# The norm of the product in eight parts, placed among the output units

## The chip, the cores and the metric

The kernel runs on one core of a Trainium2 chip. The metric is device microseconds of one execution. The kernel before takes 1781.53 us (median of three runs, 1780.02 to 1782.26).

The core has a matrix engine (PE, whose weight loads are shown apart as PEld), a vector engine (DVE), a scalar engine (ACT), a general engine (POOL) and a queue engine (SP) that only issues transfers. POOL and ACT can issue transfers too. Each engine takes its instructions in the order in which the program recorded them.

## The reference

Two layers act on a 512 x 512 picture with 64 channels. The first is a gated triangle product with a norm before it and another behind it; the second a spectral convolution with 12 x 12 modes, each on a group-normed input and added to it:

```python
x = x + _L0_conv_ref(_gn(x), ...)
x = x + _L1_conv_ref(_gn(x), L1_conv_w_real, L1_conv_w_imag)
```

What matters here is the end of the first layer:

```python
m = sequence_mask.astype(xn.dtype)
mask = (m[:, :, None] * m[:, None, :])[..., None]
...
out_gate = jax.nn.sigmoid(xn @ ogate_w + ogate_b)
out = jnp.einsum('bkjd,bkid->bijd', left, right)
out = _ln(out, onorm_w, onorm_b)
out = out @ out_w + out_b
return out * out_gate
```

The mask is zero or one for each row. Where a column is masked, the product is zero, its norm is zero and the value before the gate is the bias row alone. So the kernel ranks the rows and columns, keeps the at most 256 unmasked ones first, and computes the product for those only (the branch `compact`).

## The kernel before, in words

`compact` goes through these stages. Rows of x are gathered in ranked order and their sums taken; the two sides of the product are computed and written to `left_d` and `right_d`; the product is made for one channel after another and written to `tri_d` (64 channels x 256 x 256); then comes the loop over steps that the change touches; then the spectral part and the last stage, which adds the second layer and writes the output.

The loop over steps handles two kinds of units of eight steps each, in a hand-written order that every engine follows (`manual_schedule`).

- A **part** is an eighth of the norm of the product with its output projection. The eight parts come first (`first = 8`). A step reads half of a tile of `tri_d` (read through SP into four places, L1025), multiplies it on PE with `both`, a 64 x 128 matrix that holds the centring matrix and the output weights side by side (L1058, two instructions for each of eight matmuls, as 64 of the 128 rows each), squares the centred half on ACT (L1078) and copies the projected half to SBUF on ACT (L1079). DVE sums the squares for two steps (L1083), ACT takes the root (L1089), DVE the reciprocal (L1263) and multiplies (L1271). POOL adds the bias row (L1278), and SP writes 8 columns of the result to `u_d` (L1283), four times a part.
- An **output unit** is 32 columns of x for half of the rows, 2 MB, gathered by POOL in two transfers (L638 is the line of every gather). There are 32, two for each of 16 column groups `jc`: one for the masked rows' half (`half` 1) and one for the other. A step transposes four blocks on PE (L1038), ACT adds a mean (L1040), PE centres them (`center_x`, `c_ps`, L1045), ACT squares (L1076), DVE sums (L1083), and twelve steps behind the centring PE multiplies by the gate's weights (`gate_x`, `w_ps`, L1045), DVE multiplies by the reciprocal (L1274) and adds the gate's bias (L1280). ACT takes the sigmoid (L1221), POOL multiplies by u or by the bias row (`gated`, L1109) and adds to x (`added`, L1113), and SP stores the result into `x_h` (L1129). One unit later DVE takes the statistics for the second group norm (L1168), and PE the forward transform of the columns (L1140), whose result ACT copies (L1148) and SP writes to `modes_d`.

The loop runs transposes 13 steps ahead (`LEAD`) of the multiply by the gate's weights. At its head stands each step's PE work; x is held in five places (`RING`), z in four buffers.

u is what `u_d` holds for an output unit's 32 columns. `load_u` issues 32 reads of 64 KB in one go (L1100), each for one column whose number, a slot, is read from `slot_row` into a register of SP. The reads for the first column group go out at the step at which the first output unit begins, those for the next ones one column group ahead. A masked column's slot is at least the number of unmasked ones; slots over K = 256 are cut to K, where `u_d` holds the bias row, and below K the parts write the bias row there, the product being zero.

A reciprocal for unit or part k + 1 (L1263) is DVE's in the last step of unit k, so two of them in a row enclose eight steps.

Of the kernel before, what the change touches and what calls it, by code (L numbers as in the profile page):

```python
# [9 lines left out]
F32 = mybir.dt.float32  # L10
I32 = mybir.dt.int32
# [6 lines left out]
P = 128  # L18
# [28 lines left out]
def conv_preact_kernel(ctx: ExitStack, tc: tile.TileContext, t: dict):  # L47
# [24 lines left out]
    n_i = const.tile([1, 1], I32, name="n_i")  # L72
    with tc.tile_pool(name="ix", bufs=1) as xp, tc.tile_pool(
# [30 lines left out]
        nc.vector.tensor_copy(n_i, cum[0:1, 7:8])  # L104
        rest = xp.tile([P, 4], F32, name="rest")
# [515 lines left out]
    def compact(fc):  # L621
# [209 lines left out]
        with tc.tile_pool(name="tri", bufs=1) as trp:  # L831
# [10 lines left out]
            with tc.tile_pool(name="mk", bufs=1) as mk, tc.tile_pool(name="mkp", bufs=1, space=PSUM) as mps:  # L842
# [5 lines left out]
                nc.vector.tensor_copy(mask_s, mask_ps)  # L848
                own = mk.tile([P, 2, P], F32, name="own")
# [3 lines left out]
                nc.vector.tensor_reduce(mask_own, own, AX.X, ALU.add)  # L853
            with tc.tile_pool(name="ti", bufs=5) as ip, tc.tile_pool(name="tt", bufs=3) as tp, tc.tile_pool(
# [49 lines left out]

                for c in range(4):
                    load_sides(c)
                for c in range(-2, C):
                    if c + 2 < C:
                        turn_sides(c + 2)
                    if 0 <= c + 1 < C:  # L910
                        keep_sides(c + 1)
                    if c >= 0:
                        product(c)
                    if 4 <= c + 6 < C:
                        load_sides(c + 6)

            SIZE = 8
            LEAD = 13
            RING = 5
            first = K * 2 // 64  # L920

            units = [(jc, half) for jc in range(NJ) for half in ((1, 0) if jc < NJ - 1 else (0, 1))]
            total_g = (first + len(units)) * SIZE
            with tc.manual_schedule(), tc.tile_pool(name="late", bufs=1) as lp:
# [13 lines left out]

                order = (0, 1, 3, 4, 2)

                def place(i):
                    return places[:, i * 64 * C : (i + 1) * 64 * C].rearrange("p (n c) -> p n c", c=C)
# [47 lines left out]
                with tc.tile_pool(name="np_x", bufs=LEAD + 2) as tp, tc.tile_pool(name="np_q", bufs=2) as sqp, tc.tile_pool(  # L990
# [3 lines left out]
                ) as s1, tc.tile_pool(name="np_n", bufs=1, space=PSUM) as ps_n, tc.tile_pool(name="opf", bufs=1, space=PSUM) as ps_f, ExitStack() as products:  # L994

                    ps_y = products.enter_context(tc.tile_pool(name="np_b", bufs=2, space=PSUM))
                    ps_c = ps_w = None

                    both = lp.tile([P, P], F32, name="both")
                    for h in range(2):  # L1000
                        hs = slice(h * C, (h + 1) * C)
                        nc.vector.tensor_copy(both[hs, :C], center[hs, hs])
                        nc.vector.tensor_copy(both[hs, C:], weights["out"][hs, hs])
# [6 lines left out]

                    factors = [scratch[:, i, SIZE * 8 :] for i in range(2)]
# [5 lines left out]
                    products_t = [place(6).rearrange("p n c -> p (n c)")[:, i * 2 * N : (i + 1) * 2 * N] for i in range(4)]  # L1017

# [3 lines left out]
                    def load_product(q):  # L1022

                        for h in range(2):
                            nc.sync.dma_start(  # L1025
                                products_t[q % 4][h * C : (h + 1) * C],
                                tri_d.rearrange("c j i -> c (j i)")[:, (2 * q + h) * 2 * N : (2 * q + h + 1) * 2 * N],
                            )

                    def transpose(s):  # L1030
                        k, n = divmod(s, SIZE)
                        if k < first:
                            return
                        flat = x_of(k - first).rearrange("p n c -> p (n c)")
# [13 lines left out]
                    def centered(s):  # L1048
                        if s >= first * SIZE:
                            return times(ps_c, "c_ps", s, center_x)  # L1050

                        ps = ps_y.tile([P, 2, 4, P], F32, name="y_ps")
                        q, e = divmod(s, 2)
                        of = products_t[q % 4][:, e * N : (e + 1) * N].rearrange("p (i k) -> p i k", i=4)
                        for i in range(4):
                            for h in range(2):
                                hs = slice(h * C, (h + 1) * C)
                                nc.tensor.matmul(ps[:, h, i, :], of[hs, i, :], both[hs], start=True, stop=True)  # L1058

                        xts[s] = tp.tile([P, 4, P], F32, name="xt_c")  # L1060
                        return ps

                    def raw(s):
                        return xts[s].rearrange("p h (i c) -> p (h i) c", c=C).rearrange("p (h i) c -> p h i c", h=2)

                    def of_pair(t, e):

                        return t.rearrange("p (h e i) c -> p h e i c", h=2, e=2)[:, :, e]

                    def squared(s, cps):  # L1070
# [4 lines left out]
                        if s >= first * SIZE:  # L1075
                            nc.scalar.activation(sq, cps, AF.Square)  # L1076
                        else:
# [456 lines left out]
```

## Time and profile before

| what | value |
|---|---|
| time, median of three runs | 1781.53 us (1780.02 to 1782.26) |
| the profiled execution: its own time | 1777.78 us |
| the profiled execution: its span | 1776.0 us |
| mean granted PE clock | 0.891 |
| PE, DVE, ACT, POOL busy over the span | 88%, 80%, 53%, 53% |
| first joined matmul of the norm of the product | 624.6 us after the span's start |
| first and last centring matmul of the output units | 730.5 and 1415.6 us |
| DVE's reciprocals: 32 for output units | 0.535 us each, 748.0 to 1426.6 us |
| HBM traffic over the span | 311.60 MB read, 204.60 MB written, 291 GB/s |

A line of the timeline gives the start and the length of a run of like instructions, engine, line, operation, tiles (written <- read), shape and number; brackets give the idle time before it and what ended it. The lengths of pipelined instructions overlap: what one costs an engine that is never idle is read from start to start. A line with SPq is SP's queue: the time of issuing, not of moving the data. In a table of windows, the busy time of each engine is followed by the number of its instructions; a DMA share of 1 means that the 16 DMA engines had packets all the time.

### The profile page before, as it was taken

To read this page: it belongs to the slowest core of one execution; us is meant where nothing else is said; L and a number is where in the kernel's file an instruction comes from. 1 tells how busy PE (TensorE), PEld (TensorE's weight loads), DVE (VectorE), ACT (ScalarE), POOL (GpSimd) and SP (SyncE) were. 2 spreads that over 40 slices of the span, in tenths; PEclk is the share of its full clock that TensorE was granted. 3 is DMA by queue.
4 is the path that set the end of the run, shared out by engine and by line. 5 is a ranking of instruction groups with operands and counts; after the bars stand their busy time and mean duration, and the time that the engine had idled before them with its cause. 6 is when DMAs were issued, how large, how long until landed. Compare 5 with 4: busy or idle time off the path is not lost. (4 is left out here: it accounts for less than half of the span.)

```text
span 1776.0 us, 32619 instructions
## 1 busy us (share of the span) xinstructions
PE 1567.8 (88%) x10918; PEld 1242.0 (70%) x10918; DVE 1413.7 (80%) x2982; ACT 933.0 (53%) x1660; POOL 936.5 (53%) x695
## 2 busy tenths in 40 slices
PE   6779799997999978899999999999999977998772
PEld 5667666662899867787888888888888745665341
DVE  7989678887455568688999999999999984865451
ACT  3666566663333266676777777777777742011000
POOL 4666211111000037698999999999999881111110
PEclk9999999999899999899999999999999976555555
DMA  7999278878898789868767767776776699999999
GB/s 281 386 386 388 107 206 227 229 229 245 279 305 303 257 246 347 298 196 296 265 242 257 253 233 259 264 249 239 249 264 244 212 318 400 425 427 427 426 427 385
DMA packets 192593, 518.48 MB, mean 292 GB/s; under 512 B 37664, under 2 KB 104480, under 8 KB 151456
## 3 DMA queue, kind: packets, MB, share of 16 engines
q1 hardware_dynamic: 156112, 295.65, 47.5%
q0 software_dynamic: 32832, 218.45, 33.4%
q10 hardware_dynamic: 3472, 2.20, 0.5%
q8 instruction: 89, 1.46, 0.3%
q14 instruction: 88, 0.72, 0.1%
HBM read 311.60 MB, written 204.60 MB: 291 GB/s over the span
## 5 line engine op out<-in xcount | busy, mean ns | idle before, releaser
L1045 PE MATMUL w_ps<-gate_x,xt_c 128*128 128x128 f32 x2048 | 280.5, 281 | 30.0 <-DVE z_t L1274 28.6
L1113 POOL TENSOR_TENSOR places<-places,z_t 128x1024 f32<-128x1024 f32 x127 | 301.3, 2372 | 8.0
L1045 PEld LDWEIGHTS w_ps<-gate_x,xt_c 128*128 128x128 f32 x2048 | 252.0, 194 | 46.4 <-DVE z_t L1274 44.6
L1045 PE MATMUL c_ps<-center_x,xt_c 128*128 128x128 f32 x2048 | 277.0, 279 | 0.8 <-ACT xt_c L1040 0.4
L1045 PEld LDWEIGHTS c_ps<-center_x,xt_c 128*128 128x128 f32 x2048 | 252.8, 194 | 3.8 <-ACT xt_c L1040 3.0
L1440 PE MATMUL l_ps<-places,rinv 24*128 24x512 f32 x512 | 206.2, 1118 | 29.3 <-DVE places L1447 19.0
L1168 DVE BATCH_NORM_STATS2 stats2c<-places 128x6 f32<-128x128 f32 x1024 | 220.5, 278 | 9.9 <-POOL places L1113 9.9
L1083 DVE TENSOR_REDUCE scratch<-sq_c 128x16 f32<-128x1024 f32 x160 | 194.6, 1216 | 31.1 <-ACT sq_c L1078 16.1
L1221 ACT ACTIVATE z_t<-z_t 128x1024 f32<-128x1024 f32 x128 | 135.5, 1058 | 131.8 <-DVE z_t L1280 131.1
L1440 PEld LDWEIGHTS l_ps<-places,rinv 24*128 24x128 f32 x512 | 119.8, 302 | 110.8 <-DVE places L1447 56.9
L1278 POOL TENSOR_TENSOR z_t<-z_t,bias_row_out 128x1024 f32<-128x1024 f32 x32 | 75.6, 2363 | 226.3 <-PE y_ps L1058 202.1
L1040 ACT ACTIVATE xt_c<-t_ps,ab_xc 128x512 f32<-128x512 f32 x256 | 176.0, 688 | 11.5 <-PE t_ps L1038 10.6
L1274 DVE TENSOR_TENSOR z_t<-w_ps,rs_n 128x512 f32<-128x512 f32 x256 | 172.0, 672 | 6.2 <-PE w_ps L1045 6.1
L1076 ACT ACTIVATE sq_c<-c_ps 128x512 f32<-128x512 f32 x256 | 150.8, 589 | 31.4 <-PE c_ps L1045 30.8
L1280 DVE TENSOR_TENSOR z_t<-z_t,scratch 128x1024 f32<-128x1024 f32 x128 | 156.3, 1221 | 9.9 <-ACT rs_n L1089 3.7
L688 DVE BATCH_NORM_STATS2 stats1c<-x_ps 128x6 f32<-128x512 f32 x256 | 157.1, 682 | 7.7 <-PE x_ps L687 7.4
L1109 POOL TENSOR_TENSOR z_t<-z_t,places 128x1024 f32<-128x1024 f32 x64 | 151.8, 2371 | 14.6 <-ACT z_t L1221 14.4
L1038 PE MATMUL t_ps<-c_ident,places 128*128 128x128 f32 x1024 | 158.4, 278 | 0.0
L1038 PEld LDWEIGHTS t_ps<-c_ident,places 128*128 128x128 f32 x1024 | 118.5, 142 | 51.4 <-issue 51.4
L1447 DVE TENSOR_TENSOR places<-places,l_ps 128x512 f32<-128x512 f32 x176 | 109.3, 682 | 55.2 <-DMA places<-x_h,dst_i 42.1
L1109 POOL TENSOR_TENSOR z_t<-z_t,bias_row_out 128x1024 f32<-128x1024 f32 x63 | 149.4, 2372 | 5.8 <-ACT z_t L1221 5.5
L673 ACT COPY xc<-xg 128x128 f32 x352 | 105.0, 298 | 66.1 <-POOL xc L673 47.1
(214 smaller groups left out, 2557.0 us busy)
## 6 DMA issues: line engine op xcount, KB each, us to landing
x_h<-places SPq DMA_DIRECT2D x64, 1024.0 KB
out_x<-places SPq DMA_DIRECT2D x44, 1024.0 KB
places<-u_d SPq DMA_DIRECT2D x512, 64.0 KB
out_x<-lx_t SPq DMA_DIRECT2D x20, 1024.0 KB
rbc<-rs_d POOLq DMA_DIRECT2D x32, 512.0 KB, 7.1
left_d<-o_c SPq DMA_DIRECT2D x64, 256.0 KB
right_d<-o_c SPq DMA_DIRECT2D x64, 256.0 KB
left_raw<-left_d SPq DMA_DIRECT2D x64, 256.0 KB
```

The costliest lines, as they stand in the source:

```text
L688: nc.vector.bn_stats(stats[:, 0, 16 * (jc % quarter) + 4 * r + c, :], ps.rearrange("p i k -> p (i k)"))
L1038: nc.tensor.transpose(tps[:, i, :], flat[:, o : o + P], ident)
L1040: nc.scalar.activation(xts[s], tps, AF.Identity, bias=ab1[:, 2:3])
L1045: nc.tensor.matmul(ps[:, 2 * i : 2 * i + 2, :], xts[s][:, i, :], w, start=True, stop=True)
L1076: nc.scalar.activation(sq, cps, AF.Square)
L1083: nc.vector.tensor_reduce(totals[k % 2][:, 8 * (n - 1) : 8 * (n + 1)], sqs.pop(s // 2), AX.X, ALU.add)
L1109: nc.gpsimd.tensor_mul(zs[k, c], zs[k, c], u)
L1113: nc.gpsimd.tensor_add(xr, xr, zs.pop((k, c)))
L1168: nc.vector.bn_stats(st[k // 4][:, g, k % 4, :], x_of(k)[:, :, 2 * g : 2 * g + 2])
L1274: nc.vector.tensor_mul(z[:, 8 * odd : 8 * odd + 8, :], wps, rs)
L1280: nc.vector.tensor_add(z, z, bias_ps["ogate"].unsqueeze(1).to_broadcast([P, 16, C]))
L1440: nc.tensor.matmul(ps.rearrange("p j o -> p (j o)"), rinv[h, b, :], it[h], start=True, stop=True, tile_position=(32 * g, 0),)
```

## The change

The eight parts no longer form a stage of their own. The units of the loop stand in a list, `line`: output unit 0, parts 0, 1 and 2, output units 1, 2 and 3, part 3, output units 4 and 5, part 4, and so on, two output units to a part, up to part 7; then the other output units. The number of steps stays the same.

A part now goes through the same operations as an output unit, from the centring on. Its data come from `tri_d` through SP straight into the ring of `xt_c` tiles (17 instead of 15), 128 KB a transfer and two a step, 15 steps ahead (`EARLY`), with no transpose. The joined matrix is gone: the centring and the output weights are two matmuls over 128 rows each (L1045 of before, `times`), 12 steps apart, and the copy by ACT is gone. DVE multiplies from PSUM.

u's reads are planned (`plan_u`), two columns in each step, for 16 steps. A plan begins four steps into the slot behind the part that makes the last of the column group's u, or behind the output unit that frees the place. Since parts can now follow reads, a masked column must read the bias row whatever its slot: slots from the number of unmasked rows on are set to K. The first output unit's x is gathered in the stage of the product.

```diff
+    n_f = const.tile([1, 1], F32, name="n_f")
...
+        nc.vector.tensor_copy(n_f, cum[0:1, 7:8])
...
+                past = mk.tile([1, N], I32, name="past")
+                nc.vector.tensor_scalar(past, slot_row, n_f, float(K), ALU.is_ge, ALU.mult)
+                nc.vector.tensor_max(slot_row, slot_row, past)
...
+            line = [0, "p0", "p1", "p2"]
+            for k in range(1, len(units)):
+                line.append(k)
+                if k % 2 == 1 and k > 1 and 2 + k // 2 < PARTS:
+                    line.append(f"p{2 + k // 2}")
...
+                def load_first(r):
+                    jc, half = units[0]
+                    dst = place(order[0])[:, r * JC : (r + 1) * JC].rearrange("p j c -> p (j c)")
+                    nc.vector.memset(dst[:, :1], 0.0)
+                    gather(dst, tiles, src_i, 2 * half + r, jc)
...
+                    if c in (C // 2, 3 * C // 4):
+                        load_first(c // (3 * C // 4))
...
+                    def load_product(s):
+
+                        xts[s] = tp.tile([P, 4, P], F32, name="xt_c")
+                        o = (part_of[s // SIZE] * SIZE + s % SIZE) // 2 * 4 * N + s % 2 * N
                         for h in range(2):
                             nc.sync.dma_start(
-                                products_t[q % 4][h * C : (h + 1) * C],
-                                tri_d.rearrange("c j i -> c (j i)")[:, (2 * q + h) * 2 * N : (2 * q + h + 1) * 2 * N],
+                                xts[s][h * C : (h + 1) * C].rearrange("p i k -> p (i k)"),
+                                tri_d.rearrange("c j i -> c (j i)")[:, o + 2 * h * N : o + (2 * h + 1) * N],
                             )
...
-                        ps = ps_y.tile([P, 2, 4, P], F32, name="y_ps")
...
-                        for i in range(4):
-                            for h in range(2):
-                                hs = slice(h * C, (h + 1) * C)
-                                nc.tensor.matmul(ps[:, h, i, :], of[hs, i, :], both[hs], start=True, stop=True)
...
-                            nc.scalar.activation(of_pair(sqs[s // 2], n % 2), cps[:, :, :, :C], AF.Square)
-                            nc.scalar.copy(raw(s), cps[:, :, :, C:])
+                        nc.scalar.activation(sq, cps, AF.Square)
...
-                    def load_u(jc):
+                    waiting = []
+
+                    def plan_u(jc):
+
+                        def some(k, regs=[]):
+                            if k % 16 == 0:
+                                regs[:] = slots_of(mybir.EngineType.SP, jc, k, k + 16)
+                            for j in range(k, k + 2):
+                                slot = regs[j % 16]
+                                nc.sync.dma_start(us[jc][:, j], u_d[:, bass.ds(slot, 1)].rearrange("p o r c -> p (o r) c"))
+
                         us[jc] = place(5 + jc % 2).rearrange("p (j r) c -> p j r c", r=2)
-                        for j, slot in enumerate(slots_of(mybir.EngineType.SP, jc)):
-                            nc.sync.dma_start(us[jc][:, j], u_d[:, bass.ds(slot, 1)].rearrange("p o r c -> p (o r) c"))
+                        waiting.extend(lambda k=k: some(k) for k in range(0, JC, 2))
...
+                    for u in range(1, len(units)):
+                        at_k = max(at[u] - 3, at[u - 5] + 2 if u >= 5 else 0)
+                        loads[at_k * SIZE + 3], loads[at_k * SIZE + 6] = (u, 0), (u, 1)
...
+                    for jc in range(NJ):
+                        after = [parts_at[min(jc, PARTS - 1)]] + [at[units.index((jc - 2, 0))] for _ in range(jc >= 2)]
+                        plans.setdefault((max(after) + 1) * SIZE + 4, []).append(jc)
...
                         if 0 <= s < total_g:
-                            wps = raw(s) if k < first else times(ps_w, "w_ps", s, gate_x)
+                            wps = times(ps_w, "w_ps", s, gate_x if k in unit_of else weights["out"])
                             del xts[s]
                         if 0 <= s + LEAD - 1 < total_g:
-                            cps = centered(s + LEAD - 1)
+                            one = center_x if (s + LEAD - 1) // SIZE in unit_of else center
+                            cps = times(ps_c, "c_ps", s + LEAD - 1, one)
...
-                        if s == first * SIZE:
-                            load_u(0)
-                        if n == 4 and v % 2 == 0 and 0 <= v < len(units) - 2:
-                            load_u(v // 2 + 1)
+                        for jc in plans.get(s, ()):
+                            plan_u(jc)
+                        if waiting:
+                            waiting.pop(0)()
```

In the list, a unit's place is its slot: output unit 0 is slot 0, part 2 slot 3, output unit 1 slot 4, part 3 slot 7, output units 4 and 5 with part 4 slots 8 to 10, output unit 12 slot 20. Slot k holds steps 8k to 8k + 7. u's columns 16 to 31 for the first column group are read in steps 28 to 35, and POOL's second multiply of output unit 1 takes them in step 37.

## The prediction

> **What bounds the kernel now.** I read the stretches first, then the four engines' timelines, then SP's.
>
> Two windows, one in the product's norm and one in the output stage. Columns: window, length, busy time (instructions) of PE, PEld, DVE, ACT, POOL, granted clock, DMA share, GB/s.
>
> ```profile
> 670.00:700.00 30.00, 24.24 (x318) 21.02 (x315) 26.01 (x32) 21.10 (x43) 22.87 (x10) 1.00 1.02 347
> 950.00:1000.00 50.00, 47.79 (x397) 42.74 (x397) 49.01 (x116) 36.04 (x55) 47.45 (x23) 0.97 0.72 246
> ```
>
> The norm stage is full on the DMA engines (1.02); the output stage has DMA room (0.72) but none on DVE (98%), POOL and PE (95%). The change moves work from the first into the second.
>
> The DVE timeline: two steps of an output unit, then four reciprocals (L1263), each the last step of a slot.
>
> ```profile
> 904.17 0.87 DVE L1168 BATCH_NORM_STATS2 stats2c<-places 128x6 f32<-128x128 f32 x4
> 904.96 1.21 DVE L1083 TENSOR_REDUCE scratch<-sq_c 128x16 f32<-128x1024 f32 x1
> 906.08 0.68 DVE L1274 TENSOR_TENSOR z_t<-w_ps,rs_n 128x512 f32<-128x512 f32 x1
> 906.68 0.86 DVE L1168 BATCH_NORM_STATS2 stats2c<-places 128x6 f32<-128x128 f32 x4
> 907.46 0.67 DVE L1274 TENSOR_TENSOR z_t<-w_ps,rs_n 128x512 f32<-128x512 f32 x1
> 908.16 1.22 DVE L1280 TENSOR_TENSOR z_t<-z_t,scratch 128x1024 f32<-128x1024 f32 x1
> ...
> 641.62 0.56 DVE L1263 RECIPROCAL scratch<-rs_n 128x64 f32<-128x64 f32 x1
> 747.97 0.54 DVE L1263 RECIPROCAL rs_n<-rs_n 128x64 f32<-128x64 f32 x1
> 1010.18 0.54 DVE L1263 RECIPROCAL rs_n<-rs_n 128x64 f32<-128x64 f32 x1
> 1426.65 0.53 DVE L1263 RECIPROCAL rs_n<-rs_n 128x64 f32<-128x64 f32 x1
> ```
>
> No gaps: by starts, stats 0.79, reduce 1.12, multiplies 0.60 and 0.70, bias 1.13, so 5.12 us per two steps and, with the reciprocal, 20.95 a unit. From 641.62 to 747.97 eight parts take 106.4 us (13.3 each); units 0 to 11 take 262.2 to 1010.18. Together 368.6.
>
> PE's timeline: end of the product, a part's joined matmuls, a unit's step.
>
> ```profile
> 612.54 5.51 PE L895 MATMUL tri_c_ps<-right_t,left_t 128*128 128x256 f32 x24
> ...
> 709.00 2.05 PE L1058 MATMUL y_ps<-both,places 64*128 64x128 f32 x30 [0.24 <-DMA places<-tri_d]
> ...
> 915.40 1.06 PE L1045 MATMUL w_ps<-gate_x,xt_c 128*128 128x128 f32 x8
> 916.30 1.06 PE L1045 MATMUL c_ps<-center_x,xt_c 128*128 128x128 f32 x8
> 917.19 0.60 PE L1038 MATMUL t_ps<-c_ident,places 128*128 128x128 f32 x4
> ```
>
> Joined: 2.05/30 = 68 ns an instruction. Full-height: 0.90/8 = 112 ns.
>
> SP's queue: last write of tri_d and first read of it, last write of u_d and first read of it, then a run of u reads.
>
> ```profile
> 619.00 0.32 SPq L903 DMA_DIRECT2D tri_d<-tri_t  x1
> 621.08 22.04 SPq L1025 DMA_DIRECT2D places<-tri_d  x20
> ...
> 751.98 0.33 SPq L1283 DMA_DIRECT2D u_d<-z_t  x1
> 759.68 0.36 SPq L1100 DMA_DIRECT2D places<-u_d  x1
> ...
> 899.79 13.33 SPq L1100 DMA_DIRECT2D places<-u_d  x22
> ```
>
> A read of what was just written goes out 2.1 us (256 KB, quiet) to 7.7 us later (512 KB, others ahead); a u read costs SP 13.33/22 = 0.61 us.
>
> **The change part by part.** Removed: 64 ACT copies (L1079, 0.58 us each) and the joined matrix. ACT is 72% busy (36.04/50), so I take 0; no more than their 37 us could come back, and none while DVE sets the pace.
>
> PE per part: 16 x 8 x 68 ns = 8.7 us becomes 8 steps x (0.90 + 0.89) = 14.3. A unit is 8 x (0.90 + 0.89 + 0.44) + two transforms of 1.0 = 19.8. DVE per part: 4 x (1.12 + 0.60 + 0.70) + 0.45 = 10.1. POOL: the groups' 2.37 us go at starts 2.39 apart, so 4 x 2.39 = 9.6 a part, 8 x 2.39 and two gathers of 1.0 = 21.1 a unit. Two units and a part: PE 53.9, DVE 52.0, POOL 51.8. Before, they cost 2 x 20.95 + 13.3 = 55.2. PE now leads, so there is almost nothing to gain; I take 54.5 (PE's sum, and 55.4 if the longest engine of each slot counts: 17.0, 18.6, 19.8).
>
> The Trainium skill, "TensorE: Matmul & The Clock Gate", section "Back-to-back issue gap", gives 81 ns a matmul at 128 columns in real streams. By that a part would be 10.4 us on PE, DVE would lead at 52.0, and five groups would save another 12 us; the f32 rows here show 112 ns.
>
> Fill: PE ends the product at 618.05. Unit 0 is already there: 8 steps of 1.33 us (t and c) and one more, then four c of 0.9 for part 0, whose data can land at 624.6 as now. First reciprocal near 633.5 for 641.6: -8.
>
> Slots 0 to 3 (unit 0, parts 0 to 2), longer of PE and DVE: 14.9, 16.3, 16.5, 17.8, and 3 for slot 1, where 7 MB (part 2's reads 2, part 0's writes 2, gathers 2, a store 1) at the 347 GB/s of the first window need 20 us: 68.5. Slots 4 to 7 (units 1 to 3, part 3), the same way: 17.8 + 18.6 + 21.0 + 19.8 = 77.2. Slots 8 to 19: 4 x 54.5 + two joins of 2.7 (a slot with one takes 23.7) = 223.4. Sum 369.1, against 368.6. Slot 20 follows a part and has no new statistics for five steps: -3.5. So far -8 + 0.5 - 3.5 = -11.
>
> Now SP. A u read picks its column at run time, so it waits for every earlier u_d write, and every u_d write waits for every earlier u read; before, all 32 writes preceded all 512 reads and one such wait was paid. Now plans for u 0 start at step 20, while parts 1 and 2 still write at steps 21 to 31: write, land, four reads, land, write. One round is 0.34 + landing + 4 x 0.61 + landing. Write landing: between 2.1 and 5.8 (the wait on u_d<-z_t ends at 759.3, 7.3 us after the issue at 751.98; less two 512 KB writes ahead of it at 347 GB/s that is 4.3; 5.8 is the mean, a gather being in flight about half the time); I take 3.5, nearer the quiet row, since one write is in flight. Read landing: between 1.9 (a 32 KB copy of POOL's) and 3.0 (eight reads in flight at 0.61 allow 4.9, rarely reached); I take 2.2. Round: 8.5 us (6.8 to 11.6) for two steps that need 4.3.
>
> The skill, "DMA: Bandwidth & Descriptors", section "Anatomy of one DMA — SWDGE (gpsimd) path", puts 2.0 us of fixed cost on a DMA, mostly the receipt, plus bytes at 436 GB/s: 3.2 and 2.15, an estimated round of 8.1 and 4 us less in the sum below; no row here isolates the receipt.
>
> First chain: 5 to the first write, 6 rounds, 6 more reads (3.7), a register load (1.7): u's second half is there 61.4 us after step 20 begins; POOL then needs a gate and an add (4.8), and only then is the z buffer free that step 42 takes (four buffers, eight steps). Step 42 is due after 8.3 + 17.8 + 17.8 + 4.6 = 48.5. Stall 18 (7.5 to 36). Behind the waiting gate stand POOL's later gates and adds, for which DVE waits.
>
> Second chain: u 2 is read in steps 52 to 67, part 3 writes in 57 to 63. Behind them on SP stand part 4's tri_d reads (step 65, needed by PE at 68): 1.5 + 3 x 8.5 + 3.8 + 4 reads 2.4 + register load 1.7 + four modes_d writes 3.0 + landing 3.5 (621.08 to 624.61) = 41.4, due after 26.2: PE stalls 15 (9 to 27). The x_h stores stand in the same queue and wait for POOL's adds (220.9 us in 31 waits, all of it SP being early); behind them it has that much room, so I charge them nothing unless SP is already late. For parts 4 to 7 only two writes meet reads, and SP has five steps to catch up: 0, and some 10 each if it hasn't.
>
> Small: two gathers for unit 0 in the product stage, 2 MB or 6 us of DMA, beside a share of 0.91 there: 0, at most 6. Five small DVE instructions: 0, at most 3. The last stage is untouched.
>
> Sum: -11 + 18 + 15 = +22, so the profiled span of 1776.0 becomes 1798. The profiled execution took 1777.8, the runs' median is 1781.5; the difference on it gives 1803.5.
>
> **The rivals.** Faster: the rounds are short. For: the 2.1 us row; against: the 7.7 us one. The two stalls are 9 x round - 45 by the sums above, so below 6.2 us the -11 prevails; at 5.3 us the first vanishes, the second is 5: -6, 1775.5. Break-even, 6.2 us: 1781.5. Worse: with PE, DVE and POOL all over 95%, any late gather stops all three; units 3 and 4 were 26.4 us apart in the old order when gathers and u reads met. Groups of 60 us add 5 x 5.5 = 27: 1831. Against it: old units keep 20.97 us with POOL at 97%. That parts don't move is excluded by the queues' order.
>
> **How the numbers follow.** Forecast 0.60 (its own range 1787 to 1834 by the rounds), faster 0.20, break-even 0.08, worse 0.12. Within 0.2% is 3.6 us, about what these runs can tell. Faster 0.20, same 0.08, slower 0.72. The range from 1771 to 1832 leaves out the ends of the faster and of the worse case.
>
> **What would show it.** SP's waits: u_d writes for u reads and u reads for u_d writes, about 8.5 us apart in parts 1 to 3; POOL idle before unit 1's second gate until a u read lands, DVE idle then; PE's c_ps idle for tri_d data at part 4; first reciprocal near 633; slots 8 to 19 near 54.5 per three. Wrong if the two stalls are under 11 us together, or if the slots themselves are long without a named wait.

## The result, and the profile after

The changed kernel takes 1872.3 us (median of four runs, 1868.7 to 1872.9), the kernel before beside it 1780.8: 1.051 times as long, 95% interval 1.049 to 1.053. The forecast was 1803.5, so its sign was right and its size wrong by 69 us.

DVE's reciprocals in the timeline of the changed kernel (L1270 there), the same five places as before: start of the loop's slots, end of slots 0 to 3, of slots 4 to 7, of slots 8 to 19, and the last one.

```profile
643.51 0.54 DVE L1270 RECIPROCAL rs_n<-rs_n 128x64 f32<-128x64 f32 x1
725.29 0.54 DVE L1270 RECIPROCAL rs_n<-rs_n 128x64 f32<-128x64 f32 x1
836.63 0.53 DVE L1270 RECIPROCAL rs_n<-rs_n 128x64 f32<-128x64 f32 x1
1104.17 0.54 DVE L1270 RECIPROCAL rs_n<-rs_n 128x64 f32<-128x64 f32 x1
1517.52 0.54 DVE L1270 RECIPROCAL rs_n<-rs_n 128x64 f32<-128x64 f32 x1
```

From the first to the fourth, eight parts and twelve units take 460.7 us; before, the same work took 368.6. Behind them little changed: 413.4 us for 416.5. So all 92 us were lost in the mixed slots, 81.8, 111.3 and 267.5 us where the forecast, without its two stalls, had 68.5, 77.2 and 223.4.

Windows of the changed kernel: two of the worst slots, and one group of a part and two units (columns as in the prediction).

```profile
725.00:787.00 62.00, 41.07 (x328) 36.35 (x327) 33.02 (x53) 30.40 (x44) 32.27 (x16) 0.92 0.53 171
973.00:1039.00 66.00, 58.21 (x490) 53.47 (x487) 55.19 (x120) 41.28 (x62) 50.93 (x24) 0.97 0.74 244
```

In the first nothing is full: PE is busy for 41 of 62 us, the DMA engines for 0.53. That is waiting. In the second PE is busy for 88%, so a group of some 65 us is mostly work, with gaps of 7.8 us in all. The forecast for this group, which has a join, was 57.2.

Who waits, between 643 and 1104 us of the changed kernel (total us, times, longest), from SP's list and then from PE's:

```profile
SPq L1286 <- DMA places<-u_d: 57.9, 27, 6.3
SPq L1100 <- DMA u_d<-z_t: 41.4, 18, 4.0
SPq L1286 <- POOL z_t L1284: 34.5, 12, 6.0
SPq L1132 <- POOL places L1116: 19.9, 7, 6.6
```

```profile
PE c_ps L1061 <- DMA xt_c<-tri_d: 37.1, 12, 7.8
```

The first two lines are the turns that the prediction described: u_d's writes (L1286) wait for reads of u_d, and reads (L1100) for writes. The next two are SP held by POOL. The last is the centring of parts waiting for `tri_d`, in twelve places, where the prediction had named one.

SP's timeline shows the turns themselves, a write, four reads, a write, four reads:

```profile
709.27 0.35 SPq L1286 DMA_DIRECT2D u_d<-z_t  x1
714.11 2.78 SPq L1100 DMA_DIRECT2D places<-u_d  x4
721.93 0.35 SPq L1286 DMA_DIRECT2D u_d<-z_t  x1
724.58 1.87 SPq L1100 DMA_DIRECT2D places<-u_d  x4
```

From the write at 709.27 to the sixth at 750.64 are 41.4 us, 8.3 a turn.

And one late read of `tri_d`, on SP and on PE:

```profile
926.62 0.50 SPq L1132 DMA_DIRECT2D x_h<-places  x1
927.32 1.56 SPq L1100 DMA_DIRECT2D places<-u_d  x2
928.97 1.54 SPq L1043 DMA_DIRECT2D xt_c<-tri_d  x2
```

```profile
939.21 2.05 PE L1061 MATMUL c_ps<-c_center,xt_c 128*128 128x128 f32 x8 [5.98 <-DMA xt_c<-tri_d]
```

The reads went out three steps ahead of their matmuls, and were there 8.7 us after the last was issued (930.5 to 939.2), behind a store of 1 MB from 926.62 and gathers of 1 MB at 918.48 and 926.74.

Such a wait costs more than its length. Two windows of the same stretch, right behind the wait and a little later:

```profile
939.20:945.10 5.90, 5.89 (x28) 5.83 (x28) 4.08 (x11) 2.23 (x3) 4.98 (x4) 0.53 0.90 311
946.60:953.30 6.70, 6.70 (x62) 6.70 (x61) 4.81 (x11) 6.16 (x9) 3.43 (x3) 1.00 0.73 239
```

For 5.9 us PE worked at a granted clock of 0.53 and did 28 matmuls, where it then did 62 in 6.7 us at 1.00. The forecast has no term for this.

### The profile page after: what moved, and what is told of

It is laid out like the page before. It is cut to its first block, busy times and chain, and to the rows that moved or that the text cites. A ratio compares the mean times of both kernels' runs of the same rounds, so it can differ in the third digit from the quotient of the medians.

```text
span 1870.9 us, 32662 instructions
## 1 busy us (share of the span) xinstructions
PE 1618.4 (87%) x10918; PEld 1300.5 (70%) x10918; DVE 1413.4 (76%) x2983; ACT 922.2 (49%) x1608; POOL 934.0 (50%) x695
## 5 line engine op out<-in xcount | busy, mean ns | idle before, releaser
L1061 PE MATMUL w_ps<-gate_x,xt_c 128*128 128x128 f32 x2048 | 284.8, 284 | 35.4 <-DVE z_t L1280 34.2
L1061 PEld LDWEIGHTS w_ps<-gate_x,xt_c 128*128 128x128 f32 x2048 | 256.5, 197 | 55.8 <-DVE z_t L1280 49.5
L1073 ACT ACTIVATE sq_c<-c_ps 128x512 f32<-128x512 f32 x320 | 188.1, 591 | 155.2 <-PE c_ps L1061 154.5
L1444 PE MATMUL l_ps<-places,rinv 24*128 24x512 f32 x512 | 208.7, 1136 | 28.7 <-DVE places L1451 18.9
L1444 PEld LDWEIGHTS l_ps<-places,rinv 24*128 24x128 f32 x512 | 121.1, 306 | 111.3 <-DVE places L1451 57.4
L1112 POOL TENSOR_TENSOR z_t<-z_t,bias_row_out 128x1024 f32<-128x1024 f32 x63 | 149.1, 2367 | 98.4 <-ACT z_t L1230 98.2
L675 ACT COPY xc<-xg 128x128 f32 x352 | 105.0, 298 | 66.7 <-POOL xc L675 35.9
L640 POOL DMA_INDIRECT places<-in_x,src_i x64 | 62.6, 979 | 149.0 <-DVE left_t L907 95.9
```

The source lines that it names most:

```text
L1061: nc.tensor.matmul(ps[:, 2 * i : 2 * i + 2, :], xts[s][:, i, :], w, start=True, stop=True)
L1112: nc.gpsimd.tensor_mul(zs[k, c], zs[k, c], u)
L1444: nc.tensor.matmul(ps.rearrange("p j o -> p (j o)"), rinv[h, b, :], it[h], start=True, stop=True, tile_position=(32 * g, 0),)
```

## The experiments

Each run was timed in rounds beside the kernel before (medians of 1779 to 1785 us there). "Slots" are the twenty mixed slots in the profiled execution, from its first reciprocal (0 to 3, 4 to 7, 8 to 19, sum). Where parts stand first, the same twenty hold the same work in another order. Letters (A, B and so on) name theories; the text ahead of each run says what they stand for. The runs with a star leave out a part of the work or fetch the wrong columns, to price it.

| run | time, us | ratio to before (95%) | 0 to 3 | 4 to 7 | 8 to 19 | sum |
|---|---|---|---|---|---|---|
| before | 1780.8 | 1 | 48.5 | 57.9 | 262.2 | 368.6 |
| the change | 1872.3 | 1.049 to 1.053 | 81.8 | 111.3 | 267.5 | 460.7 |
| narrow | 1849.5 | 1.036 to 1.039 | 79.0 | 88.0 | 262.5 | 429.6 |
| actq | 1872.2 | 1.048 to 1.051 | 77.0 | 110.8 | 263.8 | 451.5 |
| both | 1855.5 | 1.039 to 1.044 | 76.8 | 88.0 | 273.7 | 438.5 |
| spread | 1775.1 | 0.994 to 0.997 | 48.2 | 58.6 | 257.3 | 364.1 |
| first | 1878.5 | 1.051 to 1.055 | 92.9 | 105.4 | 259.7 | 458.0 |
| first_narrow | 1842.3 | 1.031 to 1.035 | 74.8 | 83.3 | 260.1 | 418.1 |
| first_plain | 1808.5 | 1.014 to 1.019 | 63.2 | 66.7 | 260.1 | 390.0 |
| nobias * | 1854.0 | 1.033 to 1.041 | 87.7 | 87.9 | 255.3 | 431.0 |
| fewu * | 1833.6 | 1.025 to 1.031 | 80.1 | 83.1 | 251.8 | 415.1 |
| oneread | 2098.1 | 1.174 to 1.179 | 158.2 | 119.0 | 399.6 | 676.7 |
| noread * | 1818.8 | 1.017 to 1.022 | 69.1 | 82.8 | 248.5 | 400.4 |
| defer | 1824.7 | 1.022 to 1.026 | 71.4 | 88.6 | 252.7 | 412.7 |
| defer_moved | 1821.0 | 1.017 to 1.023 | 74.5 | 89.2 | 248.3 | 412.1 |
| nogate * | 1818.6 | 1.017 to 1.023 | 73.2 | 85.4 | 249.3 | 407.9 |
| nogate_b * | 1828.4 | 1.027 to 1.030 | 71.3 | 89.1 | 250.8 | 411.2 |
| neither * | 1801.3 | 1.007 to 1.012 | 69.1 | 82.8 | 233.7 | 385.6 |

**The turns of writes and reads (narrow).** The recorded theory, by itself.

```diff
-        nc.gpsimd.dma_start(u_d[:, K, 0, :], rows_of["out"])
+        nc.gpsimd.dma_start(u_d[:, 0, 0, :], rows_of["out"])
...
+                nc.vector.tensor_scalar(past, slot_row, float(K), None, ALU.is_lt)
+                nc.vector.scalar_tensor_tensor(slot_row, slot_row, 1.0, past, ALU.add, ALU.mult)
...
-    nc.sync.dma_start(us[jc][:, j], u_d[:, bass.ds(slot, 1)]...)
+    nc.sync.dma_start(us[jc][:, j], u_d[:, : JC * min(jc + 1, PARTS) + 1][:, bass.ds(slot, 1)]...)
...
-                                j = JC * part_of[k] + 8 * c
+                                j = JC * part_of[k] + 8 * c + 1
```

> The changed kernel, with u's bias row moved from the last place of u_d to the first, so that the reads of a column group can be declared to reach only the places that parts already written hold. The writes of part 3 then wait for no read of group 0, and no read of a group waits for a write of a later part; instructions, their order and the data are otherwise the same. Theory A, the recorded one (the turns of writes and reads on SP cost 18 us in the first four slots and about 15 at part 4): 26 to 36 us less than the changed kernel's 1872, so 1836 to 1846. Rival B (the parts' own reads of tri_d come too late, because they are issued only about three steps ahead of the matmuls that need them): less than 10 us, 1862 to 1872. Rival C (in the mixed slots PE, DVE and POOL are each nearly full, and each waits for the next): less than 10 us as well.

22.8 us less by the medians, under the 26 to 36 that A asked; 31.1 in the profiled slots, 23.3 of it in slots 4 to 7, where slot 5 falls from 35.5 to 21.4 us. The mechanism was there, near its forecast size (33 us). But the kernel is still 66 us above the one before: the larger part has another cause.

**Another queue for tri_d's reads (actq, both).**

```diff
-                            nc.sync.dma_start(
+                            nc.scalar.dma_start(
                                 xts[s][h * C : (h + 1) * C].rearrange("p i k -> p (i k)"),
```

> The changed kernel, with the parts' reads of tri_d issued from ScalarE's queue in place of SP's, at the same step; nothing else. A (turns of writes and reads of u_d on SP): the turns stay, less than 10 us gained, 1862 to 1872. B (these reads are late, as SP gets to them only after writes and stores that wait for POOL): PE's 37 us of waits for them mostly go, 30 to 45 us gained, 1827 to 1842. C (three full engines): less than 10 us.

> The two edits above together. A alone: as the first, 1836 to 1846. B alone: as the second, 1827 to 1842. A and B both, adding: 1795 to 1815, what is left being the later start of the stage (10 us) and the mixed slots' own work. C: above 1855, since neither wait is what sets the time.

Nothing gained by the first, and the two together are no better than narrow alone. That seemed to speak against B, but ACT's timeline in the second run shows why it doesn't:

```profile
900.14 11.26 ACTq L1045 DMA_DIRECT2D xt_c<-tri_d  x2
911.44 0.60 ACT L1075 ACTIVATE sq_c<-c_ps 128x512 f32<-128x512 f32 x1 [11.78 <-DMA places<-u_d]
```

ACT stood 11.8 us in issuing a read of `tri_d`, until a read of u from SP's queue had landed. The trace's records name the semaphore of each issue: the transfers of SP and ACT share eight (numbers 99 to 106), and an issue waits for the transfer that last took its number, whatever queue that was on. The read that ACT could issue only at 910.94 has 103, which SP's read of u at 902.13 had taken. So the move to ACT didn't free these reads from SP's; it stopped ACT as well. B stayed open.

**The spread fetch by itself (spread).** The kernel before, with u's later column groups fetched two columns a step.

```diff
-                        for j, slot in enumerate(slots_of(mybir.EngineType.SP, jc)):
-                            nc.sync.dma_start(us[jc][:, j], u_d[:, bass.ds(slot, 1)]...)
+                        waiting.extend(lambda k=k: some(k) for k in range(0, JC, 2))
```

> The kernel before, with one part of the change alone: the reads of u for every column group but the first are issued two columns a step instead of 32 at once. All theories: 1781 within 4 us, as the reads lead their use by a unit and SP has room there. If the spread fetch is itself a cost (SP's later commands pushed back, u late for POOL), 5 us or more above 1781.

0.43% faster than before, 0.3 to 0.6: a miss (nobody expected a gain over 4 us), and the one version here that beats both kernels. In before, SP's queue had 64 reads in a row, and x_h's stores behind them; slot 11 took 26.4 us and takes 21.4 here (the twenty profiled slots gain 4.5 in all). SP's timeline of before:

```profile
759.68 41.31 SPq L1100 DMA_DIRECT2D places<-u_d  x64
801.11 3.06 SPq L1129 DMA_DIRECT2D x_h<-places  x4
```

In the run the first store follows 38 reads, at 791.0.

So this part of the change is worth some 8 us by the medians of the same rounds, and the rest of it costs some 99.

**Parts first (first, first_narrow, first_plain).** Is it the mixing that costs, or the parts' new form? The three keep the unjoined matmuls and put all parts ahead of unit 0; the second has narrow's edit too; the third fetches u as spread does, with no read of u among the parts.

```diff
-            line = [0, "p0", "p1", "p2"]
+            line = [f"p{q}" for q in range(PARTS)] + [0]
...
-                if k % 2 == 1 and k > 1 and 2 + k // 2 < PARTS:
-                    line.append(f"p{2 + k // 2}")
```

> The changed kernel with all eight parts ahead of the first output unit, as before the change, but still with unjoined matmuls and u fetched two columns a step: everything of the change except the mixing. If the mixing is what costs (all theories here): the parts take 8 x 14.3 = 114 us where they took 106, u is fetched after the last write, so 1775 to 1800. If the unjoined matmuls or their squares cost more than their rows say, above 1820.

> Both edits together: all eight parts ahead of the first output unit, and u's bias row first, so that no read of u waits for a later part's write. In the run with the parts first alone, the parts without reads of u between took 13.7 and 15.2 us, those with them 30 to 34, in four rounds of about 8 us each. If those rounds (A) are what held it, the parts fall to about 15 us each, 70 us less than 1878: 1795 to 1815, and the difference to 1849.5 is then what the mixing costs. If unjoined matmuls are dear in themselves, above 1840.

> All eight parts ahead of the first unit, with unjoined matmuls, and u fetched as in the run of the spread fetch alone (the first column group at once after the last part, the others two columns a step beside the units): against that run, 1775, only the unjoined matmuls and what comes with them differ. The parts without reads of u between them took 13.7 to 16.4 us where they took 12.0 before, and the last two 17.5 and 17.8 with the first unit's transposes: 8 parts in about 122 to 128 us against 106: 1788 to 1800. If SP's issue of reads wasn't what took 24 us a part in the run before, but the unjoined matmuls, 1835 or more.

All three are misses, the last by 8.5 us. In first, the slots without reads of u take 13.7 and 15.2 us, as forecast, but those with them 30.4 to 33.6: a turn of 8 to 9 us for every two steps. SP's timeline:

```profile
706.26 0.35 SPq L1286 DMA_DIRECT2D u_d<-z_t  x1
...
714.86 0.35 SPq L1286 DMA_DIRECT2D u_d<-z_t  x1
```

With the turns gone (first_narrow) these slots still take 20.5 to 24.1 us. SP then issues almost without a pause, two reads of u, two of `tri_d` and half a write a step, 3 us in all:

```profile
703.48 0.86 SPq L1100 DMA_DIRECT2D places<-u_d  x2
704.43 1.09 SPq L1043 DMA_DIRECT2D xt_c<-tri_d  x2
705.62 0.54 SPq L1288 DMA_DIRECT2D u_d<-z_t  x1
706.34 1.23 SPq L1100 DMA_DIRECT2D places<-u_d  x2
```

SP is itself the bound there: from 700 to 740 us it waits 0.9 us in all, and PE 12.7 for `tri_d`. Only first_plain is a clean look at unjoined matmuls: 33 us above spread by the medians, 26.0 in the slots, 23.1 of it in the eight parts (129.9 us for 106.8). A part alone takes 16.2 us (mean of slots 1 to 5), not 14.3, with PE busy for 93%.

A kernel that doesn't mix at all, 1808.5, thus beats every version that mixes and does all the work.

**What else SP carries (fewu, oneread), and POOL's addition (nobias).** All on top of narrow.

```diff
-                            for j in range(k, k + 2):
+                            if k % 8 == 0:
+                                j = JC * min(jc, PARTS - 1) + k + 1
+                                nc.sync.dma_start(us[jc][:, k : k + 8], u_d[:, j : j + 8])
```

> The kernel with u's bias row first (1849.5), and each column group's u fetched as four transfers of eight consecutive places in place of 32 of one place each: as many bytes over the same steps, but the wrong columns. D (eight DMA semaphores in turn, 56 transfers in a group of a part and two units): 28 of 56 fall away and tri_d's reads land in time, 25 to 45 us gained, 1805 to 1825. B (tri_d's reads issued too late, whatever stands before them) and C (POOL): less than 10 us, 1840 to 1850.

> The kernel with u's bias row first (1849.5), and each step's read of tri_d as one transfer of 128 partitions in place of two of 64. D (eight semaphores in turn): 8 of 56 transfers in a group fall away, 5 to 15 us gained, 1835 to 1845. B (these reads are late because of the time that they take to land, not of their count) and C: within 5 us of 1849.5.

> The kernel with u's bias row first (1849.5), and POOL's addition of the bias to the parts left out, four of 2.37 us in each part; u then lacks the bias. C (POOL is too full in the mixed slots): POOL's work in a group of a part and two units falls from 51 to 42 us, and the groups of 65 us come down by about as much, 6 to 9 us for each of eight parts: 1780 to 1805. D (SP is held by the eight DMA semaphores that every transfer takes in turn, so that a ninth waits for the first to land): SP no longer waits for that addition, but the transfers are as many; less than 20 us gained, 1830 to 1850.

Fewu gains 16 us, between D's claim and the others'. Nobias gains nothing by the medians, and its groups of a part and two units fall by 0.6 to 2.7 us, where C asked 6 to 9: in a part's own slot PE is the full engine (18.7 of 18.7 us), not POOL. In its profile slots 8 to 19 are 7 us shorter than in narrow, and slot 2 is 11 longer, as PE waits 17.3 us for `tri_d` there. Oneread went the other way by 250 us, and not for a reason that any theory had: the single transfer from 2 x 64 rows of 2 KB moves slowly. A window of it in which little else is in flight:

```profile
1067.50:1072.00 4.50, 2.02 (x16) 1.86 (x16) 2.90 (x4) 1.54 (x2) 0.20 (x1) 1.00 0.13 49
```

49 GB/s at a DMA share of 0.13, about two of the 16 engines. It says nothing on D, which the runs thus leave unsettled as a cause by count.

**Late reads (noread, defer, defer_moved).**

```diff
+                        xts[s] = place(7)[:, 40:48].rearrange("p (i a) c -> p i (a c)", a=2)
-                        for h in range(2):
-                            nc.sync.dma_start(
```

> The kernel with u's bias row first (1849.5), with the parts' reads of tri_d left out: their matmuls take a constant that lies in SBUF, so u is wrong. L (these reads land late, behind writes and stores that wait for POOL on SP and behind 1 MB transfers on the DMA engines): 35 to 55 us gained, 1795 to 1815. S (every slot of the mix is set by its own fullest engine, PE, DVE or POOL in turn, so that the slots add up to more than each engine's sum): less than 15 us gained, above 1835.

For defer, the writes and stores go out three steps later:

```diff
-                                nc.sync.dma_start(u_d[:, j : j + 8]..., z...)
+                                due[s + 3] = (j, z)
...
-                        if n == 7 and held(0) and v < last:
-                            store(v, 0)
-                        if n == 3 and held(1) and by_age[1] < last:
+                        if n == 2 and held(1) and by_age[1] < last:
+                            store(by_age[1], 0)
+                        if n == 6 and held(1) and by_age[1] < last:
```

> The kernel with u's bias row first (1849.5), with each write of u_d and each store of x_h issued three steps later, when POOL has done its work, so that SP comes to the reads of tri_d without waiting. L: 15 to 35 us gained, 1815 to 1835. S: less than 10 us, 1840 to 1850. Below 1781 it would beat the kernel before, which neither expects.

> The last one with the gathers of x that were issued beside a part's reads of tri_d moved one slot earlier, into the part's own slot. L: another 5 to 10 us, as the reads then have fewer bytes ahead of them, 1805 to 1830. S: within 5 us of the last one, as POOL's work in its fullest slot (the second unit after a part) stays as it was.

Noread gains 31 us, under L's 35 but twice S's 15, and defer 25, as L expected. PE's waits for `tri_d` in the slots are 31.5 us in narrow, 15.1 in defer and none in noread. So more than half of it (25 of 31 us by the medians, 17 of 29 in the slots) can be had by not letting SP wait for POOL in front of these reads. Defer_moved is within 4 us of defer, inside the intervals, as S had it. With no reads at all, slots 0 to 3 take 69.1 us, for a forecast of 68.5. But slots 8 to 19 still take 248.5 where the forecast had 223.4.

**What is left (nogate, nogate_b, neither).** In noread, defer and nogate alike, the slot of unit 7, the second after part 4, takes 24.28 us. There DVE waits for POOL. Noread has POOL's first gate of unit 6, 8.7 us into that unit's slot of 16.9 us, and the wait in the next slot:

```profile
872.33 2.37 POOL L1109 TENSOR_TENSOR z_t<-z_t,bias_row_out 128x1024 f32<-128x1024 f32 x1 [5.11 <-ACT z_t L1228]
```

```profile
DVE stats2c L1168 <- POOL places L1113: 4.6, 1, 4.6
```

POOL is busy for 23.5 of the 24.28 us. Two runs took POOL work out, around that wait, on top of defer:

```diff
-                            if held(i) and (by_age[i], c) != (last, 3):
+                            if held(i) and by_age[i] in (3, 5, 7, 9, 11):
+                                pass
+                            elif held(i) and (by_age[i], c) != (last, 3):
```

> The last but one kernel (bias row first, writes and stores three steps later; 1824.7) with POOL's multiplications by u left out for the five output units 3, 5, 7, 9 and 11, each the second after a part: 4 of 2.37 us each. S, in the form that POOL sets these slots: it stands idle for about 7 us between a part and the first unit's gates and is then full for the whole of the second unit's slot; with 7 to 9 us taken out of that slot the five groups come down by 2 to 5 us each, 10 to 25 us in all: 1800 to 1815. If POOL's place in the slots doesn't matter (PE's matmuls alone set the groups), less than 5 us: 1820 to 1825.

> The same as the last run but one (1818.6), with POOL's multiplications by u's bias left out for the other units, 4, 6, 8 and 10, each the first after a part, in place of 3 to 11. S in its second form: POOL starts on such a unit's gates 8.7 us into its slot and has eight operations of 2.37 us and four gathers of 0.98 to do, 22.9 us, before DVE may take the unit's last statistics in step 3 of the next slot, which PE would reach after some 16 us; the 4 to 5 us that DVE waits there are what lengthens the second unit's slot to 24.3 us. With four operations (9.5 us) gone, that slot falls to 19 to 21 us and the four groups by 3 to 6 us each: 12 to 24 us less than 1824.7, 1800 to 1813, and DVE's waits for POOL there (21.5 us between 851 and 1038) mostly go. If POOL doesn't set these slots in this form either: 1818 to 1825, the slots of 24.3 us unchanged.

Neither run did what its theory asked. The slot in nogate: its window, then PE's and DVE's longest wait in it:

```profile
892.00:916.20 24.20, 20.85 (x173) 18.14 (x174) 18.74 (x38) 14.79 (x22) 20.09 (x11) 1.00 0.94 299
```

```profile
PE c_ps L1063 <- DMA xt_c<-tri_d: 2.3, 2, 1.5
```

```profile
DVE stats2c L1173 <- POOL places L1118: 3.9, 1, 3.9
```

and, in the same three views, in nogate_b:

```profile
893.70:917.30 23.60, 21.09 (x185) 19.02 (x184) 18.91 (x39) 15.25 (x22) 16.62 (x9) 1.00 0.85 278
```

```profile
PE c_ps L1063 <- DMA xt_c<-tri_d: 2.5, 1, 2.5
```

```profile
DVE z_t L1285 <- PE w_ps L1063: 3.6, 1, 3.6
```

In the second, DVE's wait for POOL is gone, POOL has 7 us to spare, and the slot is hardly shorter: PE now waits for `tri_d`, and DVE for PE. Noread had shown the reverse. So the last run took both away.

> Three edits at once on the kernel with u's bias row first: writes and stores three steps later, the parts' reads of tri_d left out, and POOL's multiplications left out for units 4, 6, 8 and 10. P (in the slot of the second unit after a part two waits lie side by side, PE's for tri_d and DVE's for POOL, and taking one away alone leaves the other): the slots of 23 to 25 us fall to 19 to 21, the groups of three to 56 to 58 us, the twenty slots to 375 to 388 us and the whole to 1788 to 1802. If neither sets these slots: the slots stay at 23 us or more, the whole at 1810 to 1820 as with the reads alone left out (1818.8).

The same slot's window in that run:

```profile
879.10:899.10 20.00, 19.82 (x172) 17.88 (x173) 18.85 (x39) 15.12 (x22) 16.70 (x9) 1.00 0.73 244
```

The slot falls to 19.9 us with PE busy nearly all the time, a group without a join to 56.6 (16.9 + 19.9 + 19.9), the whole to 1801.3, at the upper end of what P expected. Two waits lay side by side, and each hid the other. Against nogate_b this run changes one thing, the reads, for 25.6 us of slots. Against noread it changes two, POOL's work and the later writes and stores, so that POOL's share of these 14.8 us was argued from the waits and not measured alone. (The run also takes 16 MB of reads off the DMA engines; how much of its gain is that wasn't separated.)

## Why the prediction was wrong

Its steps, in its own order; where nothing else is said, times are those of the profiled executions.

- **Right: the sign, the turns and the end.** A turn was put at 8.5 us (6.8 to 11.6) and measured 8.3, though its terms were off: the reads followed a write by 2.3 us in four of five turns and by 4.5 in one (put at 3.5), and the next write followed the reads by 1.6 to 5.0 us (put at 2.2). The two stalls were put at 18 and 15, 33 together. Narrow took out 31: 26 in slots 2 to 7 (the first chain) and 5 in slot 8 (the second). So the mechanism was right, and that the sum came within 2 us was luck, one stall being 8 longer and the other 10 shorter. Slots behind the mix: -3.1 us for -3.5. (Two slips: the terms of the two chains give 9 x round - 43.6, not 45, so a break-even of 6.1 us, and the first stall vanishes below 5.6, not 5.3. The 8.1 us that the prediction worked out from a page were for the path of POOL's transfers, and these are SP's.)
- **Fill, -8: 10 us short.** The gathers for unit 0 ("0, at most 6") seem to have cost their bound: the product, from its first matmul to its last, takes 164.7 us in before and 164.4 in spread, 170.6 in the changed kernel, and 167 to 173 in all that gather unit 0 there. And ACT waited 7.5 us for the last write of `tri_d` before it could write the first `xt_c` tile, so that PE, with unit 0's x "already there", stood 3.0 us for ACT. From the product's end to the first reciprocal it took 18.9 us, not 15.4.
- **The step that failed: the covers costed at nothing.** "The x_h stores ... I charge them nothing unless SP is already late", and "for parts 4 to 7 ... 0, and some 10 each if it hasn't". SP was late all along, because it waits for POOL in writes and stores with `tri_d`'s reads behind them, and these have only three steps' lead over their matmuls. The prediction worked this out for one part and took the others as covered by a view in which SP is early, the one of before. Defer and noread measure it: 17 and 29 us of slots, with PE's waits for `tri_d` down from 31.5 us to 15.1 and to nothing.
- **The same step on the other side: "4 x 54.5".** The forecast took for each group little more than the sum of PE's work, and put the case of slots that stop each other at 0.12, as its worst rival. It was the case, at 63 to 66 us a group: POOL starts a unit's gates late in the short slot after a part and runs into the next. Together with the late reads this wait makes 44 us of the slots (429.6 to 385.6, narrow to neither).
- **A term that is missing: PE's clock behind a wait.** The whole of the twenty slots in the changed kernel, in narrow and in neither, with the same 3175 recorded matmuls:

```profile
643.51:1104.17 460.66, 388.41 (x3175) 354.71 (x3174) 337.29 (x691) 254.91 (x375) 325.55 (x155) 0.94 0.66 216
646.80:1076.38 429.58, 384.64 (x3175) 353.17 (x3174) 336.47 (x691) 254.56 (x375) 325.63 (x155) 0.95 0.71 234
650.24:1035.86 385.62, 370.42 (x3175) 341.70 (x3174) 334.90 (x691) 253.80 (x375) 288.79 (x139) 0.99 0.64 220
```

PE is busy for 384.6 us in narrow and 370.4 in neither, at granted clocks of 0.95 and 0.99; the clock was below 1.00 in 7 of narrow's slots and in 2 of neither's. So 14 of the 44 us weren't PE standing idle, but the same matmuls taking longer.

- **A term mis-sized: PE's work, and in one slot POOL's.** With both waits away the slots take 385.6 us, not 369.1: 16.5 too few, nearly all of it in slots 4 to 7 (82.8 for 77.2) and 8 to 19 (233.7 for 223.4). By the prediction's own terms PE's work is 8 x 14.3 + 12 x 19.8 = 352 us; in neither PE is busy for 370.4, 117 ns a recorded matmul. The row's 112 ns was near, not exact: in first_plain, slot 4 has 131 matmuls in 15.1 us of busy PE, 115 ns. Slot 5 was put at 18.6 as the longer of PE and DVE and takes 21.4 us in neither, with POOL busy for 20.8; that sum left POOL out. The figure of the Trainium skill's "TensorE: Matmul & The Clock Gate", section "Back-to-back issue gap", 81 ns, would have made the parts cheap; the f32 matmuls of the parts here took 115.

The sum: the profiled execution has a span of 1870.9 us, 72.9 above the forecast's 1798. Of these 10 are fill, 44 the waits side by side, 16.5 work, -2 the turns and 0.4 the slots behind the mix; the other 4 lie behind the last reciprocal, where the change touches nothing and the runs take 347 to 358 us. (By the medians the forecast was 68.8 us too low.) The split of the 44 between the two waits has no single answer, as each alone is worth less than both.

Even with both waits away the twenty slots take 385.6 us, 17 more than in before. With the unjoined matmuls and no mixing they take 390.0 (first_plain), and with the joined ones 364.1 (spread). So the matmuls' new form cost 26 us of slots, and the mixing, with those waits gone, gave back some 4.

The rival "faster" fell with the length of the turns. "Worse" had the right mechanism in part and too small a price: 5 groups of +5.5, 27 us, where slots 4 to 19 of narrow, without the turns, stand 50 us above the forecast.

Not settled: whether the number of transfers in turn on eight semaphores costs anything beyond the late reads (fewu's 16 us may be either); what POOL's late start is worth by itself; and what the same tests would show with a longer lead for `tri_d`'s reads, which no run tried.

## What to carry to other kernels

A queue that was early in the old order says nothing about the new one: for each transfer that is moved, list what the queue's earlier commands wait for, and give it a lead longer than their longest wait plus the landing time beside bulk transfers (here 8.7 us). A wait of PE also costs what the matmuls behind it take longer; read the granted clock of the stretch behind it. When a wait that was taken out leaves the time as it was, look in the same stretch for a second one before giving up the first; take out both. And split a change that has several parts: one line of this one, the spread fetch, was worth having alone.

## What the runs showed of the hardware

A transfer whose source is written as 2 x 64 rows ran at 49 GB/s and a DMA share of 0.13, and the whole kernel at 2098 us, where two transfers of 64 rows of the same bytes gave 1849.5. SP took 0.57 us a transfer where nothing held it (five in 2.86 us in first_narrow), and two reads of u, two of `tri_d` and half a write for each step, 3 us, were a bound of their own. Behind a wait of 6 us PE worked for 5.9 us at a granted clock of 0.53, and then at 1.00. And a queue of its own on ACT didn't make transfers independent of SP's: ACT stood 11.8 us for a read that SP had issued.
